# Turning normalized rows by DMA instead of TensorE in a mixture-of-experts kernel, with a new opening and later result-row copies

## The chip, the cores and the metric

The kernel runs on one core of one Trainium2 chip. The time is device microseconds of one execution, as the median of several runs. TensorE (PE) multiplies, VectorE (DVE) and ScalarE (ACT) do elementwise work, GpSimd (POOL) does index work and issues indirect DMAs, and SyncE (SP) issues nearly all other DMAs from one queue in program order. An instruction on any of them waits in its place, and everything behind it on the same queue waits too.

## The reference, cut to what matters

Sixteen batches of 256 rows with 256 features pass an adapter chosen by a profile number per batch, a layer norm with per-profile gain and bias, and then a feed-forward layer with one shared MLP and eight experts, of which each row uses its best two.

```python
z = relu(einsum('bsh,bhk->bsk', x, down_w[pid]) + down_b[pid])
y = x + einsum('bsk,bkh->bsh', z, up_w[pid]) + up_b[pid]
n = (y - mean(y)) * rsqrt(var(y) + 1e-5) * ln_g[pid] + ln_b[pid]
probs = softmax(n @ gate_w + gate_b)
values, indices = top_k(probs, 2);  values /= sum(values) + 1e-9
moe = sum over the two experts e of value_e * mlp(n, ew1[e], eb1[e], ew2[e], eb2[e])
out = x + n + mlp(n, sh_w1, sh_b1, sh_w2, sh_b2) + moe
```

An MLP is `gelu(n @ w1 + b1) @ w2 + b2` with 1,024 hidden features. Everything is float32.

## The kernel before, in words

Precision is kept by splitting every float32 operand of a large product into two scaled float16 parts, high and low, and adding three products (high-high, high-low, low-high). So each 128-wide chunk of a hidden layer takes six matmuls.

The kernel does not list its instructions in the order of the loops. A planner (`Plan`, lines 77 to 147) takes operations with an engine, an assumed duration, a due value `v` and dependencies, and picks again and again the one that can start first, ties going to the smaller due value. The resulting order is written out. `deps` are results waited for, `after` only fixes an order of starts, `land` says how many bytes a DMA moves (the planner moves them at `PIPE` bytes per us). On the chip each engine runs its list in order, and semaphores follow from the data that instructions touch. The constants of lines 149 to 153 are due values: `PACE` says when adapters (`A(b) = A0 + b * PA`) and shared units (`U0 + b * PU`) are due, `P_V` when the weights of experts 0 and 1 are to be prepared.

The stages, which overlap:

- *Opening* (lines 310 to 513, 1350 to 1364): constants; 28 warm-up matmuls; `profile_rows` (396 to 458) builds, for the first two batches and then for the other 14 (line 454), a one-hot matrix that adds the adapter's second bias by a matmul; `x_scales` (462 to 513) derives a power-of-two scale. `idle_pe` (1654) puts filler matmuls into planned gaps of TensorE that start before `FILL_END`.
- *Weight preparation* (`Prep`, 517 to 681) of the shared MLP (`pE`) and of each expert: two loads of 1 MB (line 541), two squares with sums on ScalarE (557), a sum over partitions on TensorE (580), small steps on VectorE, then four high parts on ScalarE (640) and four low parts on VectorE (646). Prepared experts are also stored to DRAM (671, 678), since later units load them from there. All even-numbered and early experts share one float32 buffer, `wf`.
- *Adapters*, per batch: `load_batch` (831) issues four loads on SP, of which two first read the profile number into a register; `adapter_pe` (860) does two small float32 products and adds the result to x (line 900); `adapter_ln` (915) normalizes on VectorE (926 to 965) for two batches at a time after the first two.
- *Rows in float16*, per batch: `payload` (982) makes the high part on ScalarE (988) and the low part on VectorE (993). TensorE then turns the eight 128x128 blocks against an identity into PSUM (1004), ScalarE copies them to `xlnT` (1012), and TensorE multiplies them by the gate (1023). `xlnT[b]` held the turned float32 x of the batch until the adapter's first product had read it.
- *Routing*: `route(g)` (1053), for two batches, finds the two experts and the target rows on VectorE, and POOL scatters the float16 rows to DRAM (`xslot`, line 1143), each scatter behind a one-element `memset` of `spot` (1142), and with a pause of two small instructions after every two scatters. `table` (1179) lays out blocks of rows once all are counted; its last step clears `spot` on VectorE (1273).
- *Shared units*, batches 0 to 11 (`shared`, 1391): 48 matmuls of the first layer (691), gelu (698), high and low parts of the hidden layer (706 or 708, and 712), 48 matmuls of the second (727), and an addition to the result (1396). Batches 12 to 15 follow at the very end.
- *Routed units*: 16 units of 256 rows, two for each expert, then dynamic ones that load weights from DRAM. `block_T` (1280) loads the rows with a DMA transpose (1285) and their indices (1289). `row_weights` (1296) gathers the weights of the rows, and `scatter_y` (1305) adds the result into `yacc`, a DRAM array that begins as a copy of x (`y_init`, 1468 to 1482). These copies are ordered behind the normalization of a batch (`X_GATE`).
- *End*: `yacc` is read back, added and stored (1610 to 1652).

Of the kernel before, what the change touches and what calls it, by code (L numbers as in the profile page):

```python
# [19 lines left out]
P = 128  # L20
NB = 16
# [34 lines left out]
X_FROM = 5  # L56
FILL_END, FILL = 45.0, 3.0
# [16 lines left out]
PIPE = 260e3  # L74
# [75 lines left out]
P_V = (94.34, 87.5)  # L150
PACE = (0.0, 9.24, 27.15, 14.77)
VE2 = 3.53
TV, WV, PU2, VP = 18.05, 20.48, 10.65, 1.4
# [3 lines left out]
def adapter_moe_kernel(  # L157
# [238 lines left out]
    def profile_rows():  # L396
        u32, r32, r33 = (base[0:24, NTILE - 2 - i, :] for i in range(3))
        part = base[0:24, NTILE - 6 : NTILE - 4, :].rearrange("p j d -> p (j d)").bitcast(BF16)
        part = [part[:, i * D : (i + 1) * D] for i in range(3)]
        sp = base[0:24, NTILE - 7, :]  # L400
        ki, kf, msk = sp[:, 0:3].bitcast(I32), sp[:, 4:6], sp[:, 8:11]
        idi, idf, hotf = sp[:, 16:32].bitcast(I32), sp[:, 32:48], sp[:, 48:64]
        lds = [
            plan.op(
                "ACT", 0.45,
                lambda i=i: ACT.dma_start(base[8 * i : 8 * i + 8, NTILE - 2, :], rows[:, 0:D]), 0.02,
                land=8 * 1024,
            )
            for i in range(3)
        ]  # L410
        idl = plan.op(
            "ACT", 0.45, lambda: ACT.dma_start(idi, ids.partition_broadcast(24)), 0.02, land=99
        )
# [38 lines left out]
        more = plan.op(  # L452
            "DVE", 1.9,
            lambda: V.tensor_copy(
                hot[:, 2:NB, :], hotf[:, 2:NB].unsqueeze(2).broadcast_to([24, NB - 2, P])
            ), 2.0, [h],
        )
        return [h, w], [more, w]
# [3 lines left out]
    def x_scales(deps):  # L462
# [6 lines left out]
            ), 0.0, deps,  # L469
        )  # L470
        turn = plan.op(
            "PE", 0.3, lambda: PE.transpose(pt_of("mx0")[0:3, 0:P], amx0, ident32), 0.0, [top],
            acq=[("pt", "mx0")], lat=0.2,
# [5 lines left out]
            ], 0.0, [turn], rel=[("pt", "mx0")], first=0.2,  # L479
# [5 lines left out]
            ), 0.0, [o], acq=[("pt", "mx1")], lat=0.2,  # L485
# [16 lines left out]
            ], 0.0, [spread], rel=[("pt", "mx1")],  # L502
# [14 lines left out]
    class Prep:  # L517
# [29 lines left out]
        def build(self, joint=True, bank_of="pt"):  # L547
# [84 lines left out]
            self.done = []  # L632
            for h, o in ((0, O_W1), (1, O_W2)):
                his = []
                for i in range(2):
# [21 lines left out]
                    )  # L657
                self.done.append(los)
            if self.e == E:
# [5 lines left out]
                ), v, gate[0] + gate[1], land=P * 1024,  # L665
# [72 lines left out]
    def plan_unit(  # L738
# [8 lines left out]
        for c in range(NC):  # L747
            a = ("u", k, c)
            vc = v + step * c
            g1.append(  # L750
                plan.op(
                    "PE", 0.645 if full else 0.5, lambda c=c, a=a: mm1(pa_of(a), xin(), w1, c, n), vc,
                    [*x_deps, w_deps[0]] + ([] if loose else g1[-1:]), acq=[("pa", a)], lat=0.25,
# [77 lines left out]
    def load_batch(b, v, deps):  # L831
# [6 lines left out]
        def row_load():  # L838
# [18 lines left out]
            "SP", 1.2, row_load, v + 0.3, deps, acq=[("rw", b)], land=P * 2048  # L857
# [123 lines left out]

    def payload(b):
# [16 lines left out]
        def turn():  # L999
            pt = pt_of(("x", b)).bitcast(F16).rearrange("p (l k s) -> p l k s", l=2, k=KC)  # L1000
            for l in range(2):
                for t in range(2):
                    for k in range(KC):
                        PE.transpose(  # L1004
                            pt[:, l, k, t * P : (t + 1) * P],
                            hl()[:, t, l * D + k * P : l * D + (k + 1) * P], ident,
                        )

        T = plan.op("PE", 0.46, turn, vb, [lo], acq=[("pt", ("x", b))], lat=0.3)
        tc_done[b] = plan.op(  # L1010
            "ACT", 0.95,
            lambda: ACT.activation(
                xlnT[:, b].rearrange("p l k s -> p (l k s)"), pt_of(("x", b)).bitcast(F16), AF.Copy
            ), vb, [T, z_of[b]], rel=[("pt", ("x", b))], lat=0.05,
        )
# [37 lines left out]
    def route(g):  # L1053
# [75 lines left out]
        for c in range(2):  # L1129
            for b in prev:  # L1130
# [8 lines left out]
                for t in range(2):  # L1139
                    def scat(b=b, c=c, t=t):  # L1140
                        j = 2 * b + t
                        POOL.memset(spot, 0.0)
# [10 lines left out]
                            "POOL", 1.36, scat, vg + 3.0 * c, [sli_of[g], it],  # L1153
# [142 lines left out]
    def row_weights(wq, idt, t):  # L1296
        POOL.memset(spot, 0.0)  # L1297
        POOL.indirect_dma_start(  # L1298
            out=wq[:, t : t + 1],
            out_offset=None,  # L1300
            in_=wtab[:, :],
            in_offset=bass.IndirectOffsetOnAxis(ap=idt[:, t, 0:2].bitcast(I32), axis=0),
        )

    def scatter_y(ysb, idt, t, group):
        POOL.memset(spot, 0.0)  # L1306
# [84 lines left out]
    def shared(b, v, behind=None):  # L1391
        def evac(t, mm, v, rel):
# [10 lines left out]
            [tc_done[b]], pE.done, [pE.tail1], free_hi=b >= NSH, behind=behind,  # L1403
# [3 lines left out]
    def v_of(s):  # L1407
# [11 lines left out]
        ), 40.0, land=P * PW * 2 * NNULL,  # L1419
# [9 lines left out]
    def top2_weights(v):  # L1429
# [35 lines left out]
        "SP", 0.45, lambda: SP.dma_start(wtab[2 * NT :, :], mc[:, 0, 0:2].bitcast(F32)), 60.0, land=99  # L1465
# [33 lines left out]
    def expert_unit(s, vu):  # L1499
# [29 lines left out]
        for t in range(nt):  # L1529
            wq_of[s, t] = plan.op(  # L1530
                "POOL", 1.36,
# [6 lines left out]
        def evac(t, mm, v, rel):  # L1538
            if nt == 1:
# [15 lines left out]
                "POOL", 1.9,  # L1555
# [229 lines left out]
```

## Time and profile before

| What | Value |
|---|---|
| median of 3 runs | 618.86 us (618.11 to 623.89) |
| the profiled execution, its own time | 621.28 us |
| its span, first to last instruction | 619.5 us |
| mean granted TensorE clock | 0.988 |
| first shared first-layer matmul (L691) | 29.43 us |
| first routed first-layer matmul | 205.03 us |
| last matmul group ends, by the chain | 612.26 us |
| HBM read, written | 92.41 MB, 46.58 MB |

The profile is one execution. Busy times are shares of its span; a busy TensorE is not TensorE at its peak, since matmuls are pipelined: a matmul of 256 columns is listed with 273 ns, while successive ones begin 109 ns apart. The chain of waits is followed back from the last instruction, at each step to what released it. A releaser stands behind an arrow in square brackets, with the idle time before the instruction. SPq and POOLq stand for what a queue issues.

### The profile page before, as it was taken

Reading aid. Unit: us, or ns where it says so; the run is one execution under the profiler, and the core shown is the slowest. Engines: PE = TensorE matmul, PEld = TensorE weight load, DVE = VectorE, ACT = ScalarE, POOL = GpSimd, SP = SyncE. Lnnn points to the kernel's source line nnn. Section 1 sums busy time; section 2 is a strip of 40 time slices with the busy share of each in tenths; the row PEclk is TensorE's granted clock in tenths of the full one; section 3 lists DMA queues with packets and bytes.
Section 4 is the critical chain, followed back from the end, with each engine's and each line's share of the span. In section 5 each row is a group of like instructions: output and inputs, shape, how many; then the busy total and the mean of one; then the engine's idle time right before and its main releaser. Section 6 shows DMA issues by size and latency. Waiting matters only on the chain.

```text
span 619.5 us, 15462 instructions
## 1 busy us (share of the span) xinstructions
PE 601.1 (97%) x5575; PEld 522.0 (84%) x5575; DVE 400.8 (65%) x1002; ACT 412.7 (67%) x630; POOL 318.7 (51%) x541
## 2 busy tenths in 40 slices
PE   7899999999999999999999999999999999999995
PEld 4578888777788888888888888998989888888884
DVE  7888888889884646778677443544454554545482
ACT  2678667787796768879887666666565555545561
POOL 2005868465776456484485567562747656263200
PEclk9799999999999999999999999999999999999998
DMA  8986976958432287989999898649994797932592
GB/s 271 282 293 210 292 223 199 355 162 298 186 137 79 50 300 99 310 238 243 272 305 224 268 239 158 125 104 277 287 247 55 190 285 138 321 35 26 143 356 69
DMA packets 100331, 129.30 MB, mean 209 GB/s; under 512 B 56574, under 2 KB 83862, under 8 KB 92054
## 3 DMA queue, kind: packets, MB, share of 16 engines
q1 hardware_dynamic: 84514, 110.18, 60.4%
q0 software_dynamic: 15216, 18.01, 15.4%
q8 instruction: 45, 0.74, 0.5%
q14 instruction: 40, 0.33, 0.2%
q10 hardware_dynamic: 516, 0.06, 0.1%
HBM read 92.41 MB, written 46.58 MB: 224 GB/s over the span
## 4 chain that ended last, share of the span: by engine, by line
PE 89%; ACT 3%; DVE 3%; DMA 3%; issue 1%; SPq 1%; DVEq 0%
PE bank L691 41%; PE bank L727 41%; PE bank L884 2%; PE bank L867 2%; PE bank L1004 1%; DMA wf<-in_ew_dram 1%; ACT h L698 1%; PE bank L888 1%; DVE wst L646 1%; DMA base<-in_x_dram 1%; PE bank L1023 1%; DMA wst<-in_rows_dram 1%; ACT wst L557 1%; ACT late L557 0%; DVE base L959 0%
## 5 line engine op out<-in xcount | busy, mean ns | idle before, releaser
L727 PEld LDWEIGHTS <-hh 128*128 128x128 f16 x2424 | 234.5, 98 | 30.6 <-DVE hh L712 1.8
L727 PE MATMUL bank<-wst,hh 128*128 128x256 f16 x1536 | 207.0, 273 | 0.0
L698 ACT ACTIVATE h<-bank,tst 128x256 f32<-128x256 f32 x256 | 137.3, 561 | 104.3 <-PE bank L691 92.7
L691 PE MATMUL bank<-late,wst 128*128 128x256 f16 x1536 | 202.5, 273 | 0.1
L691 PEld LDWEIGHTS <-wst 128*128 128x128 f16 x1536 | 150.1, 98 | 17.6 <-issue 0.3
L1307 POOL DMA_INDIRECT yacc<-late,idt x47 | 81.7, 1737 | 92.9 <-issue 23.6
L712 DVE SCALAR_TENSOR_TENSOR hh<-h,tst,hh 128x1024 f16<-128x1024 f32 x64 | 82.1, 1283 | 46.1 <-ACT hh L706 39.6
L1143 POOL DMA_INDIRECT xslot<-late,sli x64 | 69.5, 1085 | 77.3 <-ACT h L698 47.5
L691 PE MATMUL bank<-xlnT,wsh 128*128 128x256 f16 x768 | 103.4, 274 | 0.8 <-ACT h L698 0.7
L727 PE MATMUL bank<-wsh,hh 128*128 128x256 f16 x768 | 101.3, 273 | 1.9 <-DVE hh L712 1.2
L698 ACT ACTIVATE h<-bank,tsh 128x256 f32<-128x256 f32 x128 | 70.3, 561 | 48.9 <-PE bank L691 41.3
L1298 POOL DMA_INDIRECT wq<-wtab,idt x69 | 78.7, 1140 | 30.5 <-DMA idt<-xslot 17.7
L691 PEld LDWEIGHTS <-wsh 128*128 128x128 f16 x768 | 74.2, 98 | 11.3 <-issue 1.3
L1307 POOL DMA_INDIRECT yacc<-zT,idt x22 | 37.9, 1722 | 45.1 <-issue 9.9
L706 ACT ACTIVATE hh<-h,tst 128x1024 f16<-128x1024 f32 x46 | 52.8, 1147 | 1.4
L1292 DVE SCALAR_TENSOR_TENSOR late<-bank,tst 128x256 f32<-128x256 f32 x44 | 21.2, 483 | 40.9 <-PE bank L727 39.1
L712 DVE SCALAR_TENSOR_TENSOR hh<-h,tsh,hh 128x1024 f16<-128x1024 f32 x32 | 41.0, 1281 | 9.8 <-ACT hh L706 7.8
L706 ACT ACTIVATE hh<-h,tsh 128x1024 f16<-128x1024 f32 x30 | 34.4, 1148 | 0.8
L708 DVE TENSOR_SCALAR hh<-h,tst 128x1024 f16<-128x1024 f32 x18 | 13.9, 771 | 27.1 <-ACT h L698 23.7
L1306 POOL MEMSET spot<- 128x1 f32 x69 | 30.3, 439 | 0.0
L646 DVE SCALAR_TENSOR_TENSOR wst<-wf,prep,wst 128x1024 f16<-128x1024 f32 x20 | 25.1, 1278 | 0.8 <-ACT wst L640 0.8
L1297 POOL MEMSET spot<- 128x1 f32 x69 | 25.5, 369 | 0.0
(231 smaller groups left out, 627.2 us busy)
## 6 DMA issues: line engine op xcount, KB each, us to landing
wst<-scr SPq DMA_DIRECT2D x32, 1024.0 KB
scr<-wst SPq DMA_DIRECT2D x16, 1024.0 KB
wf<-scr SPq DMA_DIRECT2D x10, 1024.0 KB
wf<-in_ew_dram SPq DMA_DIRECT2D x6, 1028.0 KB
wf<-in_ew_dram SPq DMA_DIRECT2D x6, 1024.0 KB
wst<-in_adp_dram SPq DMA_DIRECT2D x16, 256.5 KB
xlnT<-in_xT_dram SPq DMA_DIRECT2D x16, 256.0 KB
base<-in_x_dram SPq DMA_DIRECT2D x16, 256.0 KB
```

The lines of the kernel that those rows point to most:

```text
L646: V.scalar_tensor_tensor(self.w[:, a + 2048 : b + 2048], self.wf[h][:, f], sc[:, 2 * h : 2 * h + 1], self.w[:, a:b], ALU.mult, ALU.subtract,)
L691: mm = PE.matmul(pa[:, 0:n_tok], w1[:, wl, c, k, :], xin[:, xl, k, 0:n_tok], start=i == 0, stop=i == len(seq) - 1,)
L698: ACT.activation(h32[:, c % 4, 0:n_tok], pa[:, 0:n_tok], AF.Gelu_apprx_tanh, bias=tail[:, c : c + 1], scale=tail[:, 8:9],)
L706: ACT.activation(hi, h4, AF.Copy, scale=tail[:, 9:10])
L712: V.scalar_tensor_tensor(hh[:, 1, c, 0:n_tok], h32[:, :, 0:n_tok], tail[:, 9:10], hh[:, 0, c, 0:n_tok], ALU.mult, ALU.subtract,)
L727: PE.matmul(py, hh[:, hl, k, t * P : (t + 1) * P], w2[:, wl, k, :], start=q == 0 and i == 0, stop=q == 3 and i == len(seq) - 1,)
L1143: ins = POOL.indirect_dma_start(out=xslot[:, :], out_offset=bass.IndirectOffsetOnAxis(ap=sli[:, c, j : j + 1], axis=0), in_=payb[plan.slot ...
L1292: V.scalar_tensor_tensor(ysb, py, tail[:, 10:11], tail[:, 11 : 11 + D], ALU.mult, ALU.add)
L1297: POOL.memset(spot, 0.0)
L1298: POOL.indirect_dma_start(out=wq[:, t : t + 1], out_offset=None, in_=wtab[:, :], in_offset=bass.IndirectOffsetOnAxis(ap=idt[:, t, 0:2].bit ...
L1306: POOL.memset(spot, 0.0)
L1307: ins = POOL.indirect_dma_start(out=yacc[:, :], out_offset=bass.IndirectOffsetOnAxis(ap=idt[:, t, 2:4].bitcast(I32), axis=0), in_=ysb, in_ ...
```

## The change

- In batches 6 to 14 SP issues two DMA transposes per batch, from the float16 rows in SBUF to `xlnT`, in place of eight TensorE transposes and the ScalarE copy. Batches 0 to 5 and 15 are turned as before.
- The copies of x to `yacc` are ordered behind the normalization of batches 13 to 15 rather than 5 to 15 (`X_FROM`).
- POOL's `memset` of `spot` in front of indirect DMAs becomes a `nop`.
- Opening: the profile numbers for `profile_rows` and its rows are loaded first on ScalarE's queue; the one-hot spread for 14 batches moves from VectorE to ScalarE; `x_scales` gets a later due value and is ordered behind batch 0's adapter; x loads of later batches are ordered behind the first half of the shared weights; the second half is due later, behind loads of batch 3; the shared first layer depends on each half of the low parts apart, and these two low parts are ordered behind batch 0's normalization and payload; the row load counts on the profile numbers, and three loads are ordered behind the second weight half.
- Due values, assumed durations and the planner's DMA rate change, among them the pace of adapters and shared units and the due values of experts 0 and 1.

The core of the diff:

```diff
-X_FROM = 5
-FILL_END, FILL = 45.0, 3.0
+X_FROM = 13
+FILL_END, FILL = 32.0, 3.0
-PIPE = 260e3
+PIPE = 300e3
-P_V = (94.34, 87.5)
-PACE = (0.0, 9.24, 27.15, 14.77)
-VE2 = 3.53
-TV, WV, PU2, VP = 18.05, 20.48, 10.65, 1.4
+DMA_T = range(6, 15)
+P_V = (174.91, 156.37)
+PACE = (0.0, 8.19, 26.22, 14.29)
+VE2 = 2.72
+TV, WV, PU2, VP = 16.1, 38.44, 10.59, 2.57
...
         more = plan.op(
-            "DVE", 1.9,
-            lambda: V.tensor_copy(
-                hot[:, 2:NB, :], hotf[:, 2:NB].unsqueeze(2).broadcast_to([24, NB - 2, P])
+            "ACT", 1.7,
+            lambda: ACT.activation(
+                hot[:, 2:NB, :], hotf[:, 2:NB].unsqueeze(2).broadcast_to([24, NB - 2, P]), AF.Copy
             ), 2.0, [h],
...
+            wd = w_deps[0][c // 4] if isinstance(w_deps[0], list) else w_deps[0]
...
-                    [*x_deps, w_deps[0]] + ([] if loose else g1[-1:]), acq=[("pa", a)], lat=0.25,
+                    [*x_deps, wd] + ([] if loose else g1[-1:]), acq=[("pa", a)], lat=0.25,
...
-            "SP", 1.2, row_load, v + 0.3, deps, acq=[("rw", b)], land=P * 2048
+            "SP", 1.2, row_load, v + 0.3, [*deps, idsl], acq=[("rw", b)], land=P * 2048
...
+        def turn():
+            for t in range(2):
+                SP.dma_start_transpose(
+                    out=xlnT[:, b, :, :, t * P : (t + 1) * P].rearrange("p l k s -> p (l k) s"),
+                    in_=hl()[:, t, 0 : 2 * D],
+                )
+
+        if b in DMA_T:
+            tc_done[b] = plan.op("SP", 1.0, turn, vb - 0.5, [lo, z_of[b]], land=2 * P * 1800)
+        else:
+            tc_done[b] = turn_pe(b, hl, vb, lo)
...
-                        POOL.memset(spot, 0.0)
+                        POOL.nop()
...
-    pE.ld.append(pE.load(1, 1.5))
-    pE.ld[1]["deps"], pE.ld[1]["after"] = [], [pE.ld[0], ld["rw"][1]]
-    scaled = x_scales([gbl, gwl])
+    pE.ld.append(pE.load(1, A(3) - 13.6))
...
+    pE.ld[1]["deps"], pE.ld[1]["after"] = [], [pE.ld[0], ld["x"][3], ld["wa"][3]]
+    for b in range(1, NB):
+        for k in ("xT", "x"):
+            ld[k][b]["after"].append(pE.ld[0])
...
+        if b == 0:
+            scaled = x_scales([gbl, gwl])
...
+        if bs == (0,):
+            pE.los[0]["after"].append(ln_done[0])
+            pE.los[1]["after"].append(lo_of[0])
...
-            [tc_done[b]], pE.done, [pE.tail1], free_hi=b >= NSH, behind=behind,
+            [tc_done[b]], [pE.los[:2], pE.done[1]], [pE.tail1], free_hi=b >= NSH, behind=behind,
```

`turn_pe` is the old pair of TensorE transposes and ScalarE copy, moved into a function of its own. The `memset` in front of the weight gathers and result scatters becomes a `nop` as well.

More of the change, by code (lines that the diff above doesn't have):

```diff
@@ L405, in profile_rows @@
                 "ACT", 0.45,
-                lambda i=i: ACT.dma_start(base[8 * i : 8 * i + 8, NTILE - 2, :], rows[:, 0:D]), 0.02,
+                lambda i=i: ACT.dma_start(base[8 * i : 8 * i + 8, NTILE - 2, :], rows[:, 0:D]), -0.6,
                 land=8 * 1024,
@@ L411, in profile_rows @@
         idl = plan.op(
-            "ACT", 0.45, lambda: ACT.dma_start(idi, ids.partition_broadcast(24)), 0.02, land=99
+            "ACT", 0.45, lambda: ACT.dma_start(idi, ids.partition_broadcast(24)), -0.7, land=99
         )
@@ L468, in x_scales @@
                 V.tensor_reduce(amx0[:, 2:3], gw32, AX.XY, ALU.max, apply_absolute_value=True),
-            ), 0.0, deps,
+            ), 1.15, deps,
         )
         turn = plan.op(
-            "PE", 0.3, lambda: PE.transpose(pt_of("mx0")[0:3, 0:P], amx0, ident32), 0.0, [top],
-            acq=[("pt", "mx0")], lat=0.2,
+            "PE", 0.3, lambda: PE.transpose(pt_of("mx0")[0:3, 0:P], amx0, ident32), 1.15, [top],
+            acq=[("pt", "mx0")], lat=0.2, after=[up_of[0]],
         )
@@ L478, in x_scales @@
                 lambda: V.tensor_scalar(amd[0:3, :], ident32[0:3, 0:3], amc[0:3, :], None, ALU.mult),
-            ], 0.0, [turn], rel=[("pt", "mx0")], first=0.2,
+            ], 1.15, [turn], rel=[("pt", "mx0")], first=0.2,
         )
@@ L484, in x_scales @@
                 pt_of("mx1")[:, 0:3], ones32[0:3, :], amd[0:3, :], start=True, stop=True
-            ), 0.0, [o], acq=[("pt", "mx1")], lat=0.2,
+            ), 1.15, [o], acq=[("pt", "mx1")], lat=0.2,
         )
@@ L501, in x_scales @@
                 ),
-            ], 0.0, [spread], rel=[("pt", "mx1")],
+            ], 1.15, [spread], rel=[("pt", "mx1")],
         )
@@ L631, in build @@
             self.tail1 = tail
-            self.done = []
+            self.done, self.los = [], []
             for h, o in ((0, O_W1), (1, O_W2)):
@@ L657, in build @@
                     )
+                    self.los.append(los)
                 self.done.append(los)
@@ L664, in build @@
                     tl[:, 11 : 11 + D], eb2[self.e : self.e + 1, :].partition_broadcast(P)
-                ), v, gate[0] + gate[1], land=P * 1024,
+                ), v, gate[0] + gate[1], land=P * 1024, after=[pE.ld[1]],
             )
@@ L980, in adapter_ln, with turn_pe @@
             ln_done[b] = out2[-1]
+    def turn_pe(b, hl, vb, lo):
+        def turn():
+            pt = pt_of(("x", b)).bitcast(F16).rearrange("p (l k s) -> p l k s", l=2, k=KC)
+            for l in range(2):
+                for t in range(2):
+                    for k in range(KC):
+                        PE.transpose(
+                            pt[:, l, k, t * P : (t + 1) * P],
+                            hl()[:, t, l * D + k * P : l * D + (k + 1) * P], ident,
+                        )
+        T = plan.op("PE", 0.46, turn, vb, [lo], acq=[("pt", ("x", b))], lat=0.3)
+        return plan.op(
+            "ACT", 0.95,
+            lambda: ACT.activation(
+                xlnT[:, b].rearrange("p l k s -> p (l k s)"), pt_of(("x", b)).bitcast(F16), AF.Copy
+            ), vb, [T, z_of[b]], rel=[("pt", ("x", b))], lat=0.05,
+        )
     def payload(b):
@@ L999, in turn @@
         def turn():
[L1000 to L1015, printed above, removed]
+            for t in range(2):
+                SP.dma_start_transpose(
+                    out=xlnT[:, b, :, :, t * P : (t + 1) * P].rearrange("p l k s -> p (l k) s"),
+                    in_=hl()[:, t, 0 : 2 * D],
+                )
+        if b in DMA_T:
+            tc_done[b] = plan.op("SP", 1.0, turn, vb - 0.5, [lo, z_of[b]], land=2 * P * 1800)
+        else:
+            tc_done[b] = turn_pe(b, hl, vb, lo)
         def gate():
@@ L1152, in route @@
                         plan.op(
-                            "POOL", 1.36, scat, vg + 3.0 * c, [sli_of[g], it],
+                            "POOL", 1.15, scat, vg + 3.0 * c, [sli_of[g], it],
                             after=[*sc[-1:], *pauses[-1:]],
@@ L1296, in row_weights @@
     def row_weights(wq, idt, t):
-        POOL.memset(spot, 0.0)
+        POOL.nop()
         POOL.indirect_dma_start(
@@ L1305, in scatter_y @@
     def scatter_y(ysb, idt, t, group):
-        POOL.memset(spot, 0.0)
+        POOL.nop()
         ins = POOL.indirect_dma_start(
@@ L1418, in adapter_moe_kernel @@
             SP.dma_start(nulls[:, :, 2 * D : PW], nullrow),
-        ), 40.0, land=P * PW * 2 * NNULL,
+        ), 40.0, land=P * PW * 2 * NNULL, after=[pE.ld[1]],
     )
@@ L1464, in adapter_moe_kernel @@
     wts_pad = plan.op(
-        "SP", 0.45, lambda: SP.dma_start(wtab[2 * NT :, :], mc[:, 0, 0:2].bitcast(F32)), 60.0, land=99
+        "SP", 0.45, lambda: SP.dma_start(wtab[2 * NT :, :], mc[:, 0, 0:2].bitcast(F32)), 60.0, land=99,
+        after=[pE.ld[1]],
     )
@@ L1530, in expert_unit @@
             wq_of[s, t] = plan.op(
-                "POOL", 1.36,
+                "POOL", 1.15,
                 lambda t=t: row_weights(wqb[plan.slot["wq", s]], idb[plan.slot["id", s]], t),
@@ L1554, in evac @@
             sc_last[s] = plan.op(
-                "POOL", 1.9,
+                "POOL", 1.7,
                 lambda: scatter_y(ysb(), idb[plan.slot["id", s]], t, same), v + 0.5,
```

## The prediction

> **What bounds the kernel now.** I read the page first (engines, slices, chain by line), then the chain piece by piece, then windows, and last the groups and queues that the edits touch. Engines and slices of the page:
>
> ```profile
> PE 601.1 (97%) x5575; PEld 522.0 (84%) x5575; DVE 400.8 (65%) x1002; ACT 412.7 (67%) x630; POOL 318.7 (51%) x541
> ...
> PEclk9799999999999999999999999999999999999998
> ...
> PE 89%; ACT 3%; DVE 3%; DMA 3%; issue 1%; SPq 1%; DVEq 0%
> ```
>
> TensorE carries 89% of the chain. A six-matmul group of L691 or L727 repeats every 0.655 us (0.109 us a matmul). Multiplying each window's matmul counts by such pitches shows no room between 220 and 612 us. What can be gained lies before about 205 us, where the first routed unit starts. The chain at the opening and at the end of the adapters (start, length, work):
>
> ```profile
> 9.54 7.32 DMA wf<-in_ew_dram
> ...
> 18.43 4.82 DMA base<-in_x_dram
> ...
> 26.25 0.96 PE bank L1004 x8
> ...
> 29.43 1.30 PE bank L691 x6
> ...
> 138.65 4.87 DVE wst L646 x4
> ...
> 170.68 1.99 ACT wst L557 x2
> ...
> 205.03 5.24 PE bank L691 x48
> ```
>
> The first shared matmul is at 29.43 us; from 137.5 to 184 us VectorE and ScalarE (expert preparations L646, L557 among adapters) end the waits; the routed units start at 205.03. Windows (length; PE, PEld, DVE, ACT, POOL busy; clock, DMA share, GB/s):
>
> ```profile
> 26.00:28.00 2.00, 2.00 (x12) 1.72 (x12) 1.72 (x2) 0.89 (x2) 0.00 (x0) 0.50 0.79 207
> 28.00:30.00 2.00, 2.00 (x19) 1.38 (x18) 1.11 (x6) 1.69 (x3) 0.00 (x0) 0.50 0.49 21
> ...
> 140.00:160.00 20.00, 19.06 (x194) 16.18 (x193) 19.20 (x64) 15.33 (x24) 11.48 (x22) 1.00 0.88 327
> 160.00:180.00 20.00, 18.59 (x200) 16.40 (x199) 15.74 (x55) 16.33 (x23) 17.24 (x40) 1.00 0.30 108
> 180.00:200.00 20.00, 19.46 (x176) 16.89 (x175) 11.65 (x41) 15.29 (x24) 10.98 (x26) 1.00 0.31 102
> ```
>
> After the idle TensorE of 22 to 24 us the granted clock is 0.50, just when the first turn and shared matmuls run. VectorE is nearly full at 140 to 160 and half free at 180 to 200. POOL's order at the end of the row scatters, and the one kind of row that shows a DMA transpose today (min/median/max ns on the queue):
>
> ```profile
> 185.17 0.10 POOL L1142 MEMSET spot<- 128x1 f32 x1 [2.66 <-DVE spot L1273]
> 185.43 0.98 POOL L1143 DMA_INDIRECT xslot<-late,sli  x1 [0.15 <-issue]
> 186.40 0.12 POOL L1142 MEMSET spot<- 128x1 f32 x1
> 186.71 0.98 POOL L1143 DMA_INDIRECT xslot<-late,sli  x1 [0.18 <-issue]
> ...
> L1285 SPq DMA_TRANSPOSE late<-xslot x69: 803/1229/5413, 196.8 to 539.2; - x69
> ```
>
> **The change part by part.** The sum is made against the profiled execution, 621.28 us (span 619.5 and 1.8 around it), which is 2.4 above the median of 618.86.
>
> *Turns by DMA (batches 6 to 14).* Removed: nine times eight matmuls of L1004. Two batches side by side take 0.89 us on the chain, 0.056 a matmul, so 72 x 0.056 = 4.0 us of TensorE, in 83 to 161 us, where counted work leaves it 3 to 9% room. Also gone are nine evictions L1012 of 1.02 us, 9.2 us of ScalarE. Full value is 4.0 where TensorE ends the wait; none where VectorE does (140 to 160). I take 3.5. Added: 18 transposes on SP's queue, 18 x 1.23 = 22 us of issue. Their landing from SBUF is not in the trace; the nearest is a routed block's, where the 2 KB metadata load behind the transpose is issued at 200.94 and seen by POOL by 203.14, so about 2 us after issue, perhaps more beside 1 MB loads, whose landing took 7.3 us (9.54 row). A batch's rows thus come 1 to 8 us later than by 0.45 + 1.02 on the engines. For shared units 6 to 11 this costs nothing: batch 6 is turned at 83.25 us while unit 6 starts at about 116 (counting L691), batch 11 at 126 for a unit at about 186; units 12 to 15 run at the end. The gate, routing and scatters do come later; they are treated below. On SP each transpose waits for the low half (L993), and the next batches' loads and expert weights are queued behind it. Adapter weights for batches 8 and 10 are issued at 40.33 and 59.65 for matmuls at 75.6 and 97.2, so 35 us cover this; without that cover each wait would be paid by TensorE.
>
> The Trainium skill, page "VectorE: DVE Perf Modes", sections "The three transpose paths" and "Rules for kernel authors", advises TensorE for a 128x128 turn if PSUM will do, with 390 ns against 1309 ns by DMA. By that rule 72 blocks lose 72 x 0.92 = 66 us if each were waited for. The pitch of 0.056 us in this trace and the 32 us before the first use say that this is latency beside other work; I go by the rows.
>
> *x copied later.* Sixteen DRAM copies (L1471, 0.56 us of queue each, 9 us on SP) leave 62 to 148 us, where DMA share is 0.6 to 0.9, for the time after batch 13, where it is 0.3. They are needed by the first result scatter at 219.6. Cost nothing, cover some 50 us; if late, every result scatter waits behind them on POOL. I take +1 for queueing beside transposes and expert weights (0 to +4).
>
> *Opening.* The adapter-row load no longer holds SP for the profile numbers (the register read sits at 2.08 to 2.9): about 0.8 us earlier adapter weights. The 14-batch one-hot spread (L454, 1.07 us) goes from VectorE to ScalarE, idle there; TensorE waited 1.41 us for the row after it (L449). The scale's tiny operations move behind batch 0's chain, which shortens L442 to L449 (8.19 to 12.77, 2.9 us of own work). Batch 0's last normalizing row (L965 at 22.10) stood behind two L646 of 1.2 us; these are now ordered behind it, and the first chunk group waits for one of them alone. Sum 0.8 + 1.4 + 2.4 = 4.6 on the path to 29.43, and with no idle at 22 to 24 the half clock may go too. The second weight half is issued some 5 us later, behind batches 2 and 3; its last split now ends at 30.9 and the first L727 is at 41.6, so 10 us cover it. I take -4 (from -8, all the interleaving gone, to +1, the loads only swapping places).
>
> *Preparations of experts 0 and 1 later in priority; adapters closer together.* Their 4.87 us block at 138.65 and ScalarE's 4.27 us leave a full VectorE stretch for one half free. Counted room of TensorE between 120 and 200 us is 5.9 us; I take 2 of it (from -5 to +5, since the same work returns just before it is needed).
>
> *POOL's memset becomes a nop.* Start to start of two scatters is 1.28 to 1.30 us, 0.98 of it the scatter. From 144.4 to 193.6 there are 24; a nop saves between 0 and 0.30 each, I take 0.2: 4.8 us. And the wait of 2.66 us goes, because a nop doesn't write the tile that L1273 clears. So the scatters end 7.5 us earlier (2.7 to 9.9), and DMA-turned rows of batches 12 to 14 may give some back. The first routed unit needs this: its second transpose, issued at 199.51, has landed by about 203, 2 us before 205.03. Behind 220 us the memsets of L1297 and L1306 are beside a full TensorE: nothing. The earlier prefetch of dynamic weights is nothing for the same reason.
>
> *Sum.* Supply of TensorE: -3.5 - 4 - 2 + 1 = -8.5. The routing allows at most 7.5 + 2 = -9.5 unless batches come earlier as well. I take -8: 621.3 - 8 - 2.4 = **611 us**.
>
> **Rivals.**
> *A, little.* VectorE, with only 1 us less work, stays the limit from 40 to 180 us (16 to 19 of each 20 us busy), the freed TensorE time becomes idle, and only the opening counts: 618.9 - 4 + 1 = 616. The same end results if the nop saves nothing: 2.66 of POOL and 2 of margin give 614. For it: the chain's L646 and L959 pieces; against it: L691 and L727 pieces fill it up to 136.
> *B, slower: expert 0's weights late.* A preparation takes 4.87 us plus small steps of VectorE, some 8.5 of ScalarE (two squares of 2.1, 4.27 of splits) and two 1 MB loads of up to 7 us; one buffer makes expert 1 wait for expert 0, and expert 2's (squares at 170.68) follows. If 0 and 1 both fall behind the last adapter, 13 us of VectorE must fit in the 12.6 free between 160 and 200, and the loads in front are not covered. It decides when expert 0's last L646 ends after about 197 us; with one whole preparation uncovered (15 us) it gives 618.9 - 8 + 15 = 626. Against it: its load starts at 34.8 today and can use gaps.
> *C, more.* The whole opening (-8) and full turns with earlier routing: 605.
> *D, the transposes stop SP.* If they hold adapter loads, nine waits of 1.5 us give 618.9 - 8 + 13 = 624; the 35 us of lead speak against it.
>
> **How the numbers follow.** Forecast (606 to 614) 0.52; A 0.22; C 0.10; B 0.10; D 0.06. A measurement of this kernel tells about 1% from no change: below 612.7 or above 625. Faster takes C and most of the forecast, 0.57; slower takes B and some of D, 0.12; the rest, 0.31, is the same. The range 603 to 622 holds forecast, A and C and leaves B and D out. The forecast's own range is 606 to 614.
>
> **What would show it.** First shared L691 near 25 us with a clock of 1.0; L1004 x56 instead of x128 and 18 transposes from `late` to `xlnT` at about 1.2 us; no 2.66 us wait of POOL at L1273; first routed L691 near 197 us; then the same 0.655 us groups. Wrong would be: an expert-0 split ending the wait for the first routed unit, adapters waiting for loads behind a transpose, or copies of x still landing at the first result scatter.

## The result and the profile after

The changed kernel took 621.44 us (median of 20 runs) beside 618.08 us for the kernel before on the same chip (20 runs): ratio 1.0045, 95% interval 1.0029 to 1.0060, so slightly slower. A second measurement, on another chip, gave 1.0012 (0.9984 to 1.0040), which can't be told from no change. Forecast were 611 us and a ratio of about 0.987. The profiled executions are single ones: 619.71 us for the changed kernel, below its median, and 621.28 us for before, above its median. So their spans (617.9 and 619.5 us) stand the other way round than the medians. The lines below are of the changed kernel; its line numbers are moved: L691 is now L693, L727 is L729, L646 is L647, L557 is L558, L1004 is L991.

Engines, clock and the chain by engine, from its page:

```profile
PE 596.8 (97%) x5491; PEld 517.7 (84%) x5491; DVE 395.3 (64%) x998; ACT 409.5 (66%) x625; POOL 308.8 (50%) x339
...
PEclk8799999999999899999999999999999999999999
...
PE 82%; DMA 7%; DVE 3%; SPq 3%; ACT 3%; issue 1%; ACTq 0%; DVEq 0%
```

TensorE has 4.3 us less to do (601.1 before; 4.0 were counted). But its share of the chain fell from 89% to 82%, and transfers rose from 3% to 7%: the saved work has become waiting. The clock, all 9s there before, has an 8 as its fourteenth digit, the slice at 201 to 216 us. Where the chain leaves TensorE behind the opening:

```profile
136.19 6.97 DMA xlnT<-late
...
180.00 2.45 DVE wst L647 x2
...
191.32 5.12 DMA wf<-in_ew_dram
...
198.47 1.05 ACT hh L708
...
209.06 5.09 DMA xlnT<-in_ew_dram
...
214.41 2.00 ACT late L558 x2
...
237.53 4.27 ACT wst L641 x4
...
268.01 8.18 DMA xlnT<-in_ew_dram
```

Before, the pieces of ScalarE that begin at 170.68 ended at 183.7. Then the chain was matmuls until 278 us, where ScalarE's squares and gelus hold it for some 6 us, and no load ended a wait in the routed part. Now loads of expert weights (`in_ew`) end waits until 276 us. TensorE, ScalarE and SP at the place, from three timelines (start, length, operation, idle time in front and who ended it):

```profile
188.85 0.82 PE L693 MATMUL bank<-xlnT,wsh 128*128 128x256 f16 x6
...
192.12 0.82 PE L693 MATMUL bank<-late,wst 128*128 128x256 f16 x6
...
199.56 0.61 PE L729 MATMUL bank<-wsh,hh 128*128 128x256 f16 x2 [2.69 <-ACT hh L708]
200.88 1.03 PE L729 MATMUL bank<-wsh,hh 128*128 128x256 f16 x4 [0.71 <-DVE hh L714]
221.07 0.81 PE L693 MATMUL bank<-late,wst 128*128 128x256 f16 x6 [1.38 <-ACT h L700]
```

```profile
196.46 1.91 ACT L558 ACTIVATE wst<-wf 128x2048 f16<-128x2048 f32 x1 [4.89 <-DMA wf<-in_ew_dram]
198.28 0.19 ACT L558 ACTIVATION_READ_ACCUMULATOR wst<-wf 128x1 f32 x1
198.37 1.13 ACT L708 ACTIVATE hh<-h,tsh 128x1024 f16<-128x1024 f32 x1
```

```profile
185.38 0.34 SPq L1445 DMA_DIRECT2D sb_b<-in_sb_dram  x1
186.73 1.27 SPq L1301 DMA_TRANSPOSE late<-xslot  x1
188.22 0.40 SPq L1305 DMA_DIRECT2D idt<-xslot  x1
189.36 1.22 SPq L1301 DMA_TRANSPOSE late<-xslot  x1
190.79 0.42 SPq L1305 DMA_DIRECT2D idt<-xslot  x1
191.32 0.84 SPq L542 DMA_DIRECT2D wf<-in_ew_dram  x2
```

Read from the bottom up. Expert 1's load is issued at 191.32 only: its buffer was busy with expert 0 until 183.7, and the first block's transposes, which wait for the last row scatter, stand before it on SP. ScalarE, which works in program order, stands 4.89 us in front of expert 1's first square, and the small step that finishes a hidden block (L708, behind the square) is late by that and by the square's 1.91 us. TensorE waits for L708 for 2.69 us. The first routed unit itself started at 192.12, 12.9 us earlier than before (205.03).

The wait costs more than its length. Windows around it (length; busy times; clock, DMA share, GB/s):

```profile
190.00:195.00 5.00, 5.00 (x48) 4.43 (x47) 0.48 (x1) 0.83 (x2) 1.93 (x2) 1.00 0.69 191
195.00:200.00 5.00, 2.31 (x20) 1.56 (x17) 0.78 (x3) 3.49 (x4) 0.00 (x0) 0.96 0.84 299
200.00:202.00 2.00, 1.29 (x7) 0.81 (x7) 0.82 (x1) 1.28 (x1) 0.00 (x0) 0.50 1.02 430
202.00:204.00 2.00, 2.00 (x11) 1.43 (x10) 0.00 (x0) 2.00 (x5) 0.00 (x0) 0.50 1.03 421
204.00:206.00 2.00, 2.00 (x13) 1.51 (x11) 1.39 (x9) 1.47 (x3) 0.00 (x0) 0.50 1.29 250
```

Some six microseconds at half clock follow 3.4 us of waiting (2.69 and 0.71), and half of 6 is another 3. The next table makes it visible: number the matmuls of the two MLP layers (L691 and L727, now L693 and L729) by their starts in the trace, and note how much earlier than in the trace of before the same number is reached ("lead", us). The other columns are runs of the next section. They come from chips on which before itself ran at 618 to 624 us, so read the shape of a column, not its level.

```
count  (before at)  after  after_2  a_noturn  a_pv  a_x01w  b_x01w  a_sq  a_sq8  a_pv0_lat4
  50      41.5      -1.1    -1.1     -1.6     -2.3   -1.6    +0.3   -2.0   -0.9    +0.2
 970     184.7      +8.8    +8.0     +1.4     +2.0   +8.7    +0.9   +8.3   +6.8    +5.3
1150     204.5      +8.2    +5.4     +1.6     +1.0   +8.4    +0.9   +7.6   +4.4    +2.8
1200     210.0      +1.4    -1.6     +1.6     +1.0   +8.3    +0.9   +7.4   +4.3    +2.8
1320     223.4      -0.2    -3.1     -4.3     +1.3   +6.7    +0.8   +5.2   +2.0    +3.1
1760     271.7      -1.0    -3.9     -5.2     +0.2   +5.9    +0.8   +4.7   +1.2    +3.1
1940     291.9      -1.4    -3.6     -4.8     +0.7   +5.6    +1.3   +0.3   +1.6    +3.5
4300     540.1      -1.0    -4.3     -9.6     -0.9   +4.6    +1.8   -0.3   -0.3    +4.0
4968     612.0      +0.6    -2.7     -8.1     +0.7   +6.1    +3.3   +1.3   +1.3    +5.5
```

The changed kernel leads by 8.8 us at 185 us and has lost it all by 223; 6.8 us of it go between counts 1150 and 1200, at the wait and the half clock above. So the lead was there; it was given back. (In the last row every column rises by 1.5 to 2 us: before's own trace loses them behind 540 us.)

### The profile page after: what moved, and what is told of

The parts are those of the page before. It is cut to its first block, busy times and chain, and to the rows that moved or that the text cites. A ratio compares the mean times of both kernels' runs of the same rounds, so it can differ in the third digit from the quotient of the medians.

```text
span 617.9 us, 15101 instructions
## 1 busy us (share of the span) xinstructions
PE 596.8 (97%) x5491; PEld 517.7 (84%) x5491; DVE 395.3 (64%) x998; ACT 409.5 (66%) x625; POOL 308.8 (50%) x339
## 4 chain that ended last, share of the span: by engine, by line
PE 82%; DMA 7%; DVE 3%; SPq 3%; ACT 3%; issue 1%; ACTq 0%; DVEq 0%
PE bank L729 38%; PE bank L693 38%; PE bank L887 2%; DMA xlnT<-in_ew_dram 2%; DMA gateb_b<-in_gate_b_dram 1%; PE bank L870 1%; DMA xlnT<-late 1%; SPq L1301 1%; DMA wst<-in_adp_dram 1%; DMA wf<-in_ew_dram 1%; PE bank L891 1%; DVE wst L647 1%; PE bank L1039 1%; ACT wst L641 1%; DMA base<-in_x_dram 0%
## 5 line engine op out<-in xcount | busy, mean ns | idle before, releaser
L729 PEld LDWEIGHTS <-hh 128*128 128x128 f16 x2424 | 234.9, 98 | 33.4 <-ACT hh L708 3.0
L693 PE MATMUL bank<-late,wst 128*128 128x256 f16 x1536 | 203.3, 274 | 2.7 <-ACT h L700 2.6
L729 PE MATMUL bank<-wst,hh 128*128 128x256 f16 x1536 | 205.4, 273 | 0.0
L693 PEld LDWEIGHTS <-wst 128*128 128x128 f16 x1536 | 150.7, 98 | 21.1 <-issue 3.4
L1323 POOL DMA_INDIRECT yacc<-late,idt x47 | 83.8, 1783 | 83.3 <-issue 24.2
L1314 POOL DMA_INDIRECT wq<-wtab,idt x69 | 81.7, 1184 | 66.7 <-DMA idt<-xslot 49.5
L1159 POOL DMA_INDIRECT xslot<-late,sli x64 | 75.1, 1173 | 68.1 <-DVE st L929 47.0
L729 PE MATMUL bank<-wsh,hh 128*128 128x256 f16 x768 | 104.6, 275 | 3.9 <-ACT hh L708 2.7
L693 PE MATMUL bank<-xlnT,wsh 128*128 128x256 f16 x768 | 103.0, 273 | 0.1
L693 PEld LDWEIGHTS <-wsh 128*128 128x128 f16 x768 | 74.2, 98 | 10.3 <-DVE wsh L647 0.4
L708 ACT ACTIVATE hh<-h,tst 128x1024 f16<-128x1024 f32 x47 | 53.9, 1147 | 1.4
L708 ACT ACTIVATE hh<-h,tsh 128x1024 f16<-128x1024 f32 x30 | 34.4, 1146 | 0.8
L1419 DVE SCALAR_TENSOR_TENSOR base<-bank,tsh,base 128x256 f32<-128x256 f32 x32 | 15.4, 480 | 18.6 <-PE bank L729 18.4
L647 DVE SCALAR_TENSOR_TENSOR wst<-wf,prep,wst 128x1024 f16<-128x1024 f32 x20 | 24.9, 1280 | 2.1 <-ACT wst L641 2.1
L1184 POOL IOTA sb_b<- 128x256 int32 x64 | 22.3, 348 | 2.8
```

The costliest lines, as they stand in the source:

```text
L647: V.scalar_tensor_tensor(self.w[:, a + 2048 : b + 2048], self.wf[h][:, f], sc[:, 2 * h : 2 * h + 1], self.w[:, a:b], ALU.mult, ALU.subtract,)
L693: mm = PE.matmul(pa[:, 0:n_tok], w1[:, wl, c, k, :], xin[:, xl, k, 0:n_tok], start=i == 0, stop=i == len(seq) - 1,)
L708: ACT.activation(hi, h4, AF.Copy, scale=tail[:, 9:10])
L729: PE.matmul(py, hh[:, hl, k, t * P : (t + 1) * P], w2[:, wl, k, :], start=q == 0 and i == 0, stop=q == 3 and i == len(seq) - 1,)
L1159: ins = POOL.indirect_dma_start(out=xslot[:, :], out_offset=bass.IndirectOffsetOnAxis(ap=sli[:, c, j : j + 1], axis=0), in_=payb[plan.slot ...
L1184: POOL.iota(sb2_b.bitcast(I32), pattern=[[1, D]], base=0, channel_multiplier=0)
```

## The experiments

Theory: the supply of TensorE gains some 8 us by 190 us, and the preparations put off to 175 us and later give it back, one behind another. Rivals: the routed part can't take an earlier start whatever the preparations do; or nothing of the gain came from the parts named.

**Loads earlier on SP, due times back, small loads first, no turns** (one chip).

a_ld1: expert 1's loads ordered before the first block transposes, those of experts 2 and 3 behind later blocks.

```diff
+    sb2_ld["after"].append(prep[1].ld[1])
-            after=[last] if s >= NS else [], acq=[("xg", s), ("id", s)], land=nt * P * 1024,
+            after=[last] if s >= NS else [prep[1].ld[1]], acq=[("xg", s), ("id", s)], land=nt * P * 1024,
...
+            if e in (2, 3):
+                prep[e].ld[0]["after"].append(BT[5 - e])
```

> The changed kernel with one order forced on SP: the two weight loads of expert 1 go ahead of the first routed rows and the late bias load, and the loads of experts 2 and 3 keep their places behind routed rows. Theory 1 (the 8 us lead that the changed kernel has at 196 us is lost because expert 1's load stands on SP behind routed rows that wait for POOL's scatters, issued at 191.3, and its square stands on ScalarE in front of the gelu chain): the load is issued near 184, the 2.7 us wait at 196.9 and the half clock behind it go, and the time falls by 4 to 8 us to 613 to 617. Rival (DMA transposes and loads on the 16 engines are the cause, or the work of the late preparations itself): 619 to 622, with the wait moved to another place.

Measured 1.0072 (1.0043 to 1.0101): no gain. Expert 1's load left at 185.75 and its wait was gone, but the next one came (ScalarE, then TensorE):

```profile
218.02 1.91 ACT L558 ACTIVATE late<-xlnT 128x2048 f16<-128x2048 f32 x1 [7.78 <-DMA xlnT<-in_ew_dram]
```

```profile
218.86 0.61 PE L729 MATMUL bank<-wst,hh 128*128 128x256 f16 x2 [5.01 <-DVE hh L710]
```

Moving one load moves the wait to the square of another expert, expert 3.

a_pv: `P_V = (174.91, 156.37)` back to `(94.34, 87.5)`, all else as changed.

> The changed kernel with the old due values of the preparations of experts 0 and 1, 94.34 and 87.5. Theory 1: the stretch 196 to 221 has no wait for expert 1's weights, but the preparations return among the adapters and take 2 to 4 us of the lead there: 614 to 618. Rival (the work of the preparations costs the same wherever it stands): 619 to 622.

Measured 0.9970 (0.9937 to 1.0004): not told from before, and 0.4 to 0.75% below the changed kernel, 2.6 to 4.6 us (against 1.0012 the intervals overlap). Its lead is only 2.0 at 185 us, and still 1.3 at 223. It differs from the changed kernel in these due times alone, so some 7 of the 9 us of lead at 185 us are there only because the preparations are put off.

a_gw: the priorities of ScalarE's first loads back (-0.6 and -0.7 to 0.02), so gate weights and gains come first.

> The changed kernel with the old order of small loads on ScalarE's queue (gain, bias and gate weights before the rows and profile numbers). In the changed kernel the gate weights are issued at 4.65 and reach VectorE at 11.8, and the one-hot bias chain stands behind them, so TensorE waits 6.1 us. Theory on the opening: the wait falls below 1.5 us, the first shared matmul comes 3 to 5 us earlier; the lead grows by as much until 190, but the end gains only 0 to 4 us (617 to 621) because the wait at 196 is set by POOL and expert 1. Rival (the rows of the adapters, not the gate weights, are late): first shared matmul unchanged, 621.

Measured 1.0022 (0.9997 to 1.0048); first shared matmul at 28.36 us (28.80 in the changed kernel, 29.29 before, all by the timeline). One late load took the place of another, as VectorE's timeline shows, first of the changed kernel, then of a_gw:

```profile
11.77 0.17 DVE L469 TENSOR_REDUCE amx<-gw 128x1 f32<-128x16 f32 x1 [5.63 <-DMA gw<-in_gate_w_dram]
```

```profile
9.80 0.16 DVE L434 CAST base<-base 24x16 f32<-24x16 int32 x1 [4.27 <-DMA base<-in_ids_dram]
```

In both it is the sixth load of ScalarE's queue, issued at 4.65 and 4.70 when x had landed, 8 KB or 1.5 KB behind a 1 MB load.

a_noturn: `DMA_T = range(0)`, so all batches are turned on TensorE.

> The changed kernel with all batches turned on TensorE as before. Theory 1: the turns by DMA save TensorE 3 to 4 us and harm nothing, so the time rises by 2 to 5 us to 623 to 626. Rival (the transposes on SP hold the queue and delay gates and routing): the time falls below 620.

Measured 1.0134 (1.0082 to 1.0186). Against the changed kernel's 1.0045 and 1.0012 the turns are worth 0.9 to 1.2%, 5.5 to 7.5 us, in this setting (each to about half a per cent, so 3.5 us isn't excluded), and the lead at 185 us is 1.4 in place of 8.0 to 8.8. The loss behind 204 us is there without the turns as well.

**Preparations left out** (first pair disturbed).

> The changed kernel unaltered, beside the runs that it is compared with here. Both theories: ratio to before 1.003 to 1.006.

Measured 1.0012, as told above.

a_x01 and b_x01 left out the preparations of experts 0 and 1 in the changed kernel and in before, with their weight tiles zeroed by GpSimd:

```diff
+            if self.e == E and h == 1:
+                POOL.memset(wst[0], 0.0)
+                POOL.memset(wst[1], 0.0)
```

> The changed kernel with the preparation of experts 0 and 1 left out: no loads, squares or splits of their weights; their weight tiles are zeroed by GpSimd before 30 us, the order of everything else is kept. If the gain of the supply is given back because the late preparations come back one behind another between 177 and 285 us, this runs 8 to 12 us below before (ratio 0.980 to 0.988) and no square ends a wait between 195 and 215 us. If the routed part could not take an earlier start whatever the preparations do, the collapse of the lead at 196 to 221 us stays and the ratio is 0.995 to 1.005.

> The kernel before with the same preparations left out, as the measure of what they cost there. If they only stall TensorE among the adapters at 105 to 185 us: 2 to 6 us faster, ratio 0.990 to 0.997, so that the changed kernel without them is 5 to 8 us faster than this one. If what the change gives back does not hang on them, the two kernels without them differ as the two with them do, the changed one 2 to 4 us slower.

Measured 1.0038 (1.0007 to 1.0069) and 1.0129 (1.0089 to 1.0170): slower with less work. Neither theory had this. The timelines of GpSimd and VectorE in b_x01:

```profile
3.69 6.91 POOL L551 MEMSET wst<- 128x8192 f16 x1
10.55 6.91 POOL L552 MEMSET wst<- 128x8192 f16 x1
```

```profile
3.91 13.58 DVE L353 TENSOR_SCALAR mine<-mine 128x8 f32<-128x8 f32 x1
```

An operation of 0.18 us (the same step's in the changed kernel) lasted until the memsets ended, and with it the opening. These two runs say nothing on the question. Done again with the units of experts 0 and 1 reading the shared weights, so that nothing is filled:

```diff
-            self.w = wsh if e == E else wst[e % NBUF]
+            self.w = wsh if e == E or e < 2 else wst[e % NBUF]
```

> The changed kernel with the preparation of experts 0 and 1 left out once more, now without a GpSimd memset: their units multiply by the shared expert's weights, so no load, square or split of theirs is made; all else keeps its order. If the gain of the supply is given back because the late preparations come back one behind another: 8 to 12 us below before, ratio 0.980 to 0.988. If the routed part cannot take an earlier start: 0.995 to 1.005, with the lead still lost at 196 to 221 us.

> The kernel before with the same left out. First theory: 2 to 6 us faster than before (0.990 to 0.997), and the changed kernel without them 5 to 8 us faster than this. Second: the changed one without them is no faster than this one.

Measured 0.9876 (0.9848 to 0.9903) for the changed kernel, 0.9929 (0.9903 to 0.9956) for before. Without the two preparations the changed kernel is 3.3 us faster than before without them, by the ratios (the medians are 612.46 and 616.25 us); with them it was 0.7 to 2.8 us slower. The lead of 8.7 at 185 us is still 8.3 at count 1200: the routed part does take the earlier start. That is less than the 5 to 8 us expected, and 2.5 us of the lead still go between 204 and 272 us: TensorE waits there for gelus behind the squares of expert 3 (1.02 us) and the splits of expert 2 (0.48 us).

**Which part of a preparation.** a_sq and b_sq let the squares of experts 0 to 3, and VectorE's small maximum, read long-landed tiles, in the changed kernel and in before; a_sq8 does so for all eight (`E` for `4`). The scales of these experts then don't come from their weights; all else is computed.

```diff
-                        self.junk, self.wf[h][:, 0:2048], AF.Square,
+                        self.junk, (wsh if self.e < 4 else self.wf[h])[:, 0:2048], AF.Square,
```

> The changed kernel with one wait taken away: the squares (and the small maximum) of experts 0 to 3 read tiles that are long there, in place of the loaded weights, so ScalarE does the same work in the same order but the square doesn't wait for the load (the scales are then wrong). First theory, with the square in front of the gelu as the place: TensorE's waits at 197 to 222 us go, 3 to 6 us less than the changed kernel, ratio to before 0.993 to 0.998. Rival: the wait moves to the splits behind the load or to the weight gathers, ratio as the changed kernel's, 1.001 to 1.005.

> The kernel before with the same squares freed of the load. Both theories: its loads are early, nothing to gain, 0.998 to 1.001.

> The squares (and the small maximum) of all eight experts read tiles that are long there, not those of experts 0 to 3 alone; the scales are then wrong. With experts 0 to 3 freed, the lead over before stayed at 5.5 us until 265 us and was lost there in front of expert 5's square. If it is the square that waits for a load in front of the gelus, whichever expert's, the lead of 4 to 6 us now stays to the end: ratio 0.989 to 0.993. If what is lost moves on to another wait (a block's transpose, splits behind the load): 0.996 to 1.000.

Measured 0.9983 (0.9957 to 1.0008), 0.9986 (0.9964 to 1.0007) and 0.9932 (0.9909 to 0.9955). In a_sq the lead passes 210 us nearly whole; 4.4 us of it are lost where the first square that still waits stands, expert 5's:

```profile
275.33 2.46 PE L693 MATMUL bank<-late,wst 128*128 128x256 f16 x12 [2.98 <-ACT h L700]
```

With all eight freed it isn't lost there. The work is the same, instruction for instruction; only what the first steps wait for differs. So the wait for a load in front of the steps of the running units, on ScalarE (and perhaps VectorE: the two were freed together), gives back 0.8 to 1.1%, 5 to 7 us. Each ratio is known to 0.2 or 0.3%, and the changed kernel itself didn't run on a_sq8's chip: the ratios to before carry the comparison. At the wait of 2.69 us it was ScalarE: VectorE was past its small maximum at 196.8 and stood 2.72 us for L708. The rest of the lead that a_sq8 loses, from 6.8 to 2.0 at 185 to 223 us, goes with a wait of 1.67 us behind a square itself and one of 2.43 us for a block's transpose; these weren't taken apart:

```profile
195.88 0.81 PE L693 MATMUL bank<-late,wst 128*128 128x256 f16 x6 [1.67 <-ACT wst L558]
...
211.05 4.09 PE L693 MATMUL bank<-late,wst 128*128 128x256 f16 x36 [2.43 <-DMA late<-xslot]
```

**A cure.** The idea is that the plan counts an expert's load as landed too early. a_lat4 counts 4 us more; a_pv0 gives expert 0 alone its old due time; a_pv0_lat4 does both; a_pv_lat4 has both old due times and the 4 us; b_lat4 is before with the 4 us.

```diff
-P_V = (174.91, 156.37)
+P_V = (94.34, 156.37)
...
+                lat=4.0 if self.e < E else 0.0,
```

> The changed kernel with one number of the plan altered: an expert's load counts as landed 4 us later, so the plan puts squares and splits later among ScalarE's and VectorE's work; all is computed. First theory: most waits for a load at 196 to 222 us and 268 to 278 us go, ratio 0.992 to 0.999. Rival: splits come later and TensorE waits for the weights of a unit, 1.000 to 1.006.

> The changed kernel with the old due time of expert 0 alone (94.34 for 174.91): its buffer comes free near 105 us in place of 184, so the loads of experts 1 and 2 are issued before the routed units start. First theory: no square ends a wait at 196 to 210 us; the lead is 3 to 6 us there and stays: ratio 0.991 to 0.997. Rival: as with both due times old, what is saved behind 196 us is paid among the adapters, lead 2 us, 0.996 to 1.000.

> Both alterations together. First theory: no loss behind 196 us nor at 265 to 285 us, 0.988 to 0.995, the fastest so far of those that compute everything. Rival: 0.996 to 1.002.

> The kernel before with the same number of the plan altered: an expert's load counts as landed 4 us later. Its loads are issued early and no square waits in the routed part, so if the number only cures waits that the change brought: ratio 0.998 to 1.004. If it is a gain of its own, independent of the change: 0.992 to 0.997.

> The changed kernel with both old due times of the preparations and the altered landing number; against the kernel before with that number it shows what the rest of the change (turns, copies of x, opening, GpSimd's nop) is worth with the preparations where they were. Theory: turns worth some 5 us, nothing lost: 0.990 to 0.996. Rival: the preparations among the adapters take it back, 0.997 to 1.002.

```
a_lat4      1.0115 (1.0078 to 1.0151)     b_lat4     1.0099 (1.0076 to 1.0122)
a_pv0       0.9980 (0.9951 to 1.0009)     a_pv_lat4  0.9944 (0.9923 to 0.9965)
a_pv0_lat4  0.9930 (0.9904 to 0.9955)
```

a_pv0_lat4 computes everything and beats both kernels: 617.38 us beside 623.25 for before on its chip. Its chain is TensorE's again, and the stretch that was at half clock runs full:

```profile
PE 89%; DMA 4%; ACT 3%; DVE 2%; SPq 1%; issue 1%; ACTq 0%; DVEq 0%
```

```profile
200.00:205.00 5.00, 5.00 (x48) 4.48 (x46) 0.48 (x1) 2.42 (x5) 1.90 (x2) 1.00 0.29 53
```

The old due time of expert 0 alone (a_pv0) isn't told from before. The 4 us alone cure nothing: with late due times (a_lat4) the splits of experts 2 and 3 run one behind the other on ScalarE, and TensorE waits 4.13 us for a gelu behind them, not for the weights that the rival named:

```profile
252.35 5.08 PE L694 MATMUL bank<-late,wst 128*128 128x256 f16 x30 [4.13 <-ACT h L701]
```

In before (b_lat4) they cost 1% too, against both expectations. Its lead goes from 0.4 to -6.1 between counts 1150 and 1200: its first routed unit waits 3.45 us, by the chain behind a block's transpose that leaves SP at 202.2 (196.8 in before), and the clock behind the wait is 0.50. What holds the transpose was not pursued:

```profile
208.08 8.16 PE L692 MATMUL bank<-late,wst 128*128 128x256 f16 x47 [3.45 <-POOL spot L1298]
```

With the old due times and the same 4 us in both, the changed kernel is 1.5% faster (0.9944 against 1.0099), so that number isn't a gain of its own.

**One part alone.** b_turn: before with the turns by DMA, and nothing else.

> The kernel before with one part of the change alone: batches 6 to 14 turned by DMA. If the turns are worth what the changed kernel lost without them, some 5 us: ratio 0.991 to 0.995. If they pay only with the rest (SP's queue also carries the copies of x at 62 to 148 us here, and VectorE stays the limit): 0.998 to 1.005.

Measured 1.0412 (1.0365 to 1.0459), 25 us slower, outside both. SP, GpSimd and TensorE in b_turn:

```profile
161.04 28.92 SPq L1021 DMA_TRANSPOSE xlnT<-late  x4
```

```profile
134.50 0.30 POOL L1137 IOTA late<- 128x2 int32 x3 [17.89 <-DMA xlnT<-late]
```

```profile
229.48 2.93 PE L692 MATMUL bank<-late,wst 128*128 128x256 f16 x13 [15.97 <-DMA late<-xslot]
```

With SP's order as before, the last transpose leaves at 188.6 us (147.1 in the changed kernel), GpSimd waits 37.5 us in three places for buffers that transposes still read, and the routed units start at 229.5. TensorE was still 1.9 us ahead of before at 198 us. Which of the other edits protects the turns (copies of x later, due times, the planned DMA rate) was not tried, and neither were those due values and that rate by themselves in the changed kernel, other than the two of `P_V`.

## Why the prediction was wrong, point by point

*What bounds the kernel.* Right. All that the change gained lay before 205 us, and without the two late preparations (a_x01w) most of it stays to the end.

*Turns: -3.5.* Right in kind, probably too small: 5.5 to 7.5 us, in this setting. I counted TensorE's 4 us and gave ScalarE's nine evictions no price; whether they make the difference was not tried. As a part alone the turns cost 25 us, so "35 us of lead cover SP" held for the loads but not for what waits behind the turn itself. Rival D, given 0.06, had the transposes stop SP and hold adapter loads; in b_turn they stopped SP, but what they held up were GpSimd's scatters.

*Opening: -4.* Wrong: by the timeline the first shared matmul came at 28.80 instead of 29.29, and the half clock stood at 12 to 22 us, where before it stood at 14 to 17 and at 25 to 31. I added up gaps on engines, though from 8 to 26 us the DMA share is 0.8 to 1.2 in both kernels, and loads make up 16.6 of the first 23.3 us of before's chain and 17.6 of the first 25.0 of the changed one's. So I read the opening as one that waits for bytes; no run took that apart. a_gw, which put another late load in place of the one visible, gained 0.4 us there.

*Copies of x, nop, routing.* Right in the number, in part by luck. The 2.66 us wait is gone and the scatters end 10 us earlier (184.6, 194.6 before; I had 7.5, at most 9.9), and the first routed unit starts at 192.1 where I said 197. Two scatters still stand 1.28 to 1.30 us apart, as before: where the memset was, 0.30 us of idle is now, so the nop saved nothing per scatter, where I had counted 4.8 us. Besides the 2.66 us, two longer waits in front of GpSimd's scatters went (8.72 and 7.34 us, at 120.7 and 144.4; behind 120 us the longest is now 2.42). What each gave of the 10 us wasn't taken apart.

*Preparations later: -2 (from -5 to +5).* This is the step that failed. I wrote that the same work returns just before it is needed, and priced it by VectorE's and ScalarE's busy time. Putting them off did buy some 7 us of lead by 185 us (8.8 against 2.0 in a_pv), but the price of their return was a wait, and I had no term for it. a_sq8 puts 5 to 7 us on loads that aren't there when ScalarE reaches their square. In net, a_pv puts 2.6 to 4.6 us on the later due times alone, and a_x01w against b_x01w 4.0 to 6.1 us on the two preparations in the changed kernel, beyond what they cost in before. The term should have stood at +3 to +6, near or beyond my own upper end of +5, with the half clock that follows a wait included.

*Rival B.* The mechanism was there (one buffer, loads uncovered, expert 1 behind expert 0) with the wrong point of decision. I let it hang on expert 0's last split, "after about 197"; that ended at 183.7, in time, and the loss came all the same, through experts 1, 3 and 5. The point to ask for was when the next load can be *issued*, and which step of ScalarE stands behind its first reader. Its price, 15 us, was too high.

Without the two preparations the rest of the change gained 3.3 us in place of the 6.5 that the sum gave it (3.5 and 4, less 1); the preparations cost 4.0 to 6.1 us in place of gaining 2. Together that is 9 to 11 us, the distance between forecast and result (10.4). Within the rest the opening is 3.5 us short; what took the surplus of the turns is open.

## What to carry to other kernels

Before you move work to a later time, ask not how much time its engines have left there but what its first instruction waits for, and what stands behind that instruction on its engine. In a kernel whose engines run in program order, one early-placed reader of a late load stops everything behind it, and the wait moves on to the next load when one is repaired. When a large gain vanishes, compare the times at which equal counts of matmuls are reached: it shows where it is given back. A lead found that way can be work put off as well as work saved.

## What the runs showed of the hardware

- A GpSimd memset of 128 x 8192 two-byte elements took 6.91 us, and VectorE stood still through two of them (13.58 us for an operation of 0.18 us). The Trainium skill, page "SBUF — State Buffer", section "Who interferes with whom", says that VectorE's `tensor_scalar` can take the port pair that it shares with GpSimd, and that the later one blocks fully; this row agrees. The two memsets follow each other without a pause.
- A wait of TensorE of 2.43 us (a_sq8, at 211 us) or 2.36 us (a_sq, at 208 us) left the granted clock at 1.00; one of 2.69 us followed by 0.71 us, or of 2.98 us (a_sq, at 275 us), was followed by 0.50 for up to 7 us. One of 2.23 us (a_noturn, at 305 us) was followed by 0.50 too, so the length of the single wait doesn't decide it. The Trainium skill, page "TensorE: Matmul & The Clock Gate", section "What's actually happening", has the clock halve after an idle window of about 3.4 us; here less was enough.
- The reverse of the first point, in the changed kernel: a row scatter of GpSimd (0.98 us in the median of 64, above 1.2 us in nine) lasted 5.21 us while VectorE made expert 0's splits (and 4.60 us in after_2, beside the same splits). Of GpSimd, then of VectorE:

```profile
178.07 0.98 POOL L1159 DMA_INDIRECT xslot<-late,sli  x1 [0.16 <-issue]
179.36 5.21 POOL L1159 DMA_INDIRECT xslot<-late,sli  x1 [0.30 <-issue]
```

```profile
178.73 1.27 DVE L647 SCALAR_TENSOR_TENSOR wst<-wf,prep,wst 128x1024 f16<-128x1024 f32 x1
...
182.45 1.27 DVE L647 SCALAR_TENSOR_TENSOR wst<-wf,prep,wst 128x1024 f16<-128x1024 f32 x1
```

  Here it is the last scatter, the one that SP's first block transpose waits for, so the late splits cost some 4 us there too. In a_pv, where the splits stand earlier, no scatter behind 173 us takes more than 1.4 us, and one at 116.6 us, beside splits (L647) and other two-input rows, takes 5.39 us. That the one causes the other is read from such rows and not tried by itself.
- A DMA turn of 128 x 512 took 1.20 to 2.46 us on SP's queue; a pair issued from 134.8 to 137.4, behind five copies of x (256 KB each) and in front of ten more, had landed at 143.2 only (the 6.97 us piece of the chain).
